# An FFN that takes 512 tokens at a time, with two of its weight matrices streamed from DRAM

## The chip, the core and the metric

The kernel runs on one core of a Trainium2 chip. The metric is the device time of one execution in microseconds (us), lower is better. The engines are TensorE (PE, with its weight loads shown apart as PEld), VectorE (DVE), ScalarE (ACT), GpSimd (POOL) and SyncE (SP), which issues the DMAs here. All inputs are float32.

## What is computed

Two blocks with adaLN modulation follow each other on `x` of shape [4, 2048, 256]. The first is a gated delta-rule memory with 4 heads of 64, which runs over chunks of 64 tokens with a state `S` per head. The second is an FFN with a SwiGLU layer and two GELU layers of width 1024. Its weights are ternary (-1, 0, 1) with a scale per output.

```python
h = _layernorm(x) * (1 + ca) + sa
x = x + ga * memory(h)          # below, per chunk
h = _layernorm(x) * (1 + cb) + sb
x = x + gb * ffn(h)

def step(S, inp):               # one chunk of the memory
    A_i, v_i, wk_i, rkg_i, wkg_i, intra_i = inp
    v_new = A_i @ v_i - (A_i @ wk_i) @ S
    o_i = rkg_i @ S + intra_i @ v_new
    S = gamma_C * S + wkg_i @ v_new

def ffn(x):
    h = silu(lin(x, w1_w, w1_s)) * lin(x, w2_w, w2_s)     # 256 -> 1024
    h = gelu(lin(h, h1_w, h1_s))                          # 1024 -> 1024
    h = gelu(lin(h, h2_w, h2_s))                          # 1024 -> 1024
    return lin(h, w3_w, w3_s)                             # 1024 -> 256
```

`A_i` is the inverse of a unit triangular 64 x 64 matrix of the chunk's keys.

## The kernel before

A step is one chunk of 64 tokens of all four batch elements, so 256 tokens; there are 32 steps. The FFN of step `s` runs beside the recurrence of chunk `s + 1` and the chunk-local matrices of chunk `s + 2`.

All FFN weights lie on the chip in float32r (`fw1`, `fw2`, `fh1`, `fh2`, `fw3`, lines 103 to 107). An activation is kept as two float32r parts whose sum is exactly the activation (`split`, line 366), so every product takes two passes. `Ffn` (line 395) emits a layer in chunks of 128 outputs. `product` (line 425) emits the matmuls of such a chunk: the weights are the stationary operand (128 x 128), the activations stream past with 256 columns. `gated` has 4 + 4 matmuls and puts both products into one PSUM bank; ACT takes Silu of the first (line 441), DVE multiplies (442), and the split is a cast on ACT (367) and a subtraction on POOL (368). `hidden` has 16 matmuls, Gelu on ACT (450), a cast on ACT and a subtraction on DVE. `last` (453) has the activations as the stationary operand and `fw3` streaming with 256 columns. The pool `pf` (line 84) has three PSUM banks for all of these.

The rest of a step is called from the loop over `s` (line 658) at fixed places. `local_keys` makes the keys of chunk `s + 2` and their transposes, `local_grams` the 64 x 64 products; their masked result goes to DRAM and comes back as `U` (lines 248 to 250). `local_inverse` inverts the diagonal blocks of 32 on DVE, 31 times two instructions (258 and 260); `local_blocks` stores the result and loads it as `E` (266, 270). `local_merge1` and `local_merge2` complete the inverse on TensorE. `rec_state`, `rec_values`, `rec_update` and `rec_out` are the recurrence. `ffn_norm` and `ffn_turn` make the input `hs` of the next FFN step, `local_norms` the input of the memory.

Each engine works through its own queue. A planner lays out the queues when the program is built, by its own estimate of when each instruction's operands are ready (line 738). `tc.issue_after(f.end)` keeps what stands under it behind the FFN's last matmul so far on TensorE, and only there. All DMAs are issued by SyncE (`move`, line 144) and so stand in one queue. PSUM has `ps2` with two buffers of two banks, `ps1` with one of two banks, and `pf`.

In the set-up (from line 471) each FFN weight is fetched in pieces of 512 KB (`fetch`, 22 of them, eight buffers), cast to float32r on ACT (line 595), and compared with the original on DVE (`compare`, 526), with a count on TensorE. The flag that comes out picks one of two versions of all steps (line 710): float32r if no weight changed, else float32. Nothing inside this branch can be placed ahead of it. Ahead of it stand the matrices and the recurrence of chunk 0 and the first FFN norm.

Of the kernel before, what the change touches and what calls it, by code (L numbers as in the profile page):

```python
"""Two blocks with adaLN modulation on one core: a gated delta-rule memory over chunks of 64 tokens, and an FFN
(SwiGLU and two GELU layers).

A step is one chunk of 64 tokens of all four batch elements 2*n + b. With tokens on partitions, b has partitions
64b..64b+63 and n lies along the free axis. With features on partitions, head 2*p + h has partitions 64h..64h+63 and
(p, n, b) lie along the free axis. The [64, 64] matrices between the tokens of a chunk lie by [tokens of b, (h, p, n)].

The FFN of a step runs beside the recurrence of the next one and the chunk-local matrices of the one after that.

An FFN weight that float32r holds exactly needs one pass for each of the two float32r parts of an activation, whose  # L10
sum is exactly the activation. Whether all of them are such is found out on the chip; if not, the FFN runs in float32.
"""
# [23 lines left out]
# Columns of the constants: what stays, then what only the set-up needs.  # L36
# [6 lines left out]
def constants():  # L43
    """By the shapes alone: indices and masks over the positions of a tile."""
    i = np.arange(P)
    t = (i % C)[:, None]
    col = np.arange(C)[None, :]
    out = np.zeros((P, NCONST), np.float32)
    out[:, IDENT:IDENT + P] = np.eye(P)
    # Row 4 * n + (partition // 32) of the identity.  # L50
    unit = np.zeros((P, 8, K), np.float32)
    for n in range(8):
        unit[i, n, 4 * n + i // K] = 1.0
    out[:, UNIT:UNIT + 8 * K] = unit.reshape(P, -1)
    out[:, DIFF:DIFF + C] = np.maximum(col - t, 0)
    out[:, STRICT:STRICT + C] = col > t
    out[:, PROW:PROW + C] = np.arange(C)
    out[:, TAIL] = C - 1 - i % C
    return out


def over(ap, dim, n):
    """`ap` with a dimension of n that repeats it."""
# [6 lines left out]
def adaln_block_kernel(ctx: ExitStack, tc: tile.TileContext, x_in, ww, wr, decay, log_alpha, w1, w2, h1, h2, w3, scol,  # L70
# [7 lines left out]
    N = B * C  # L78
# [26 lines left out]
    fh1 = cp.tile([P, NH, HID], FR, name="fh1")  # L105
    fh2 = cp.tile([P, NH, HID], FR, name="fh2")
# [4 lines left out]
    ys = [cp.tile([P, 2, D], F32, name=f"y{n}") for n in range(4)]  # L111
# [16 lines left out]

    nc.vector.memset(half, -0.5)
# [10 lines left out]
    def after(name):  # L140
        """What follows is issued behind what was marked last, on its engine."""
        return tc.issue_after(mark[name])
# [10 lines left out]
    def load(s):  # L153
        for b in range(2):
            move(out=ys[s % 4][C * b:C * b + C],
                              in_=x_in[b::2, s * C:(s + 1) * C, :].rearrange("q t d -> t q d"))

    def moments(x):
        """The mean of each token, and one over its deviation."""
# [11 lines left out]
    def local_norms(s):  # L171
        x, rk = ys[s % 4], rks[s % 2]
# [14 lines left out]
    def local_residual(s, h=None):  # L187
        x, h = ys[s % 4], hid if h is None else h
        # x becomes x + ga * h.
# [4 lines left out]
    def local_keys(s, first=False):  # L194
# [14 lines left out]
        # The write keys, a token behind, with tokens on partitions.  # L209
# [20 lines left out]
    def local_grams(s):  # L230
        IT, NMT = ITs[s % 2], NMTs[s % 2]
        # The heads h are row tiles, each with a bank of its own.
# [20 lines left out]
    def local_inverse(s, j0, j1):  # L253
        """Rows of the inverse of the diagonal blocks of 32: partition (g, block, unit), row 4 * c + g at c."""
# [18 lines left out]
    # E = [[EA, EA NMT EB], [0, EB]], of the blocks of 32.  # L273
# [79 lines left out]
    def rec_out(s, oT):  # L353
        y = ys[s % 4]
# [10 lines left out]
    def split(to, a, eng=None):  # L365
        """`a` is exactly the sum of the two parts of `to`."""
# [3 lines left out]
    def ffn_norm(s, xn=None):  # L370
        y = ys[s % 4]
# [6 lines left out]
    def ffn_turn(s, xn, fp, exact):  # L378
# [4 lines left out]
        hm = ap.tile([P, NK, B, C], F32, tag="hm", name="hm")  # L383
        for k in range(NK):
            for b in range(B):
                nc.scalar.activation(hm[:, k, b, :], tp[:, k, b // 2, C * (b % 2):C * (b % 2) + C], AF.Identity,  # L386
                                     bias=modT[:, k, b:b + 1], scale=modT[:, 2 + k, b:b + 1])
        hm = hm.rearrange("q k b t -> q k (b t)")
        if not exact:
            return hm.unsqueeze(1)  # L390
        hs = fp.tile([P, 2, NK, N], FR, tag="hs", name="hs", bufs=1)
        split([hs[:, 0], hs[:, 1]], hm)
        return hs

    class Ffn:
        """The FFN of step s: `part` emits a chunk of 128 outputs of a layer."""

        def __init__(self, s, hs, fp, exact):
            self.s, self.a, self.fp, self.exact = s, hs, fp, exact
# [3 lines left out]
        def weights(self, w, src, o, n):  # L403
            """The columns of a layer's weights that give outputs o .. o + n."""
            if self.exact:
                return w[:, :, o:o + n]
# [4 lines left out]
        def acts(self, o):  # L411
            if o == 0:
                self.next = self.fp.tile([P, self.parts, NH, N], FR if self.exact else F32, tag="act", name="act")
            to = self.next[:, 0, o, :]
# [4 lines left out]
        def done(self, o, to, eng=None):  # L419
            if self.exact:  # L420
                split([self.next[:, 0, o, :], self.next[:, 1, o, :]], to, eng)
# [3 lines left out]
        def product(self, ps, w, lhs_is_w=True, at=None):  # L425
            k_n = w.shape[1]
            for k in range(k_n):
                for i in range(self.parts):
                    a = self.a[:, i, k, :] if at is None else self.a[:, i, k, at]
                    wk = w[:, k, :]  # L430
                    self.end = nc.tensor.matmul(  # L431
                        ps, lhsT=wk if lhs_is_w else a, rhs=a if lhs_is_w else wk,
                        start=k == 0 and i == 0, stop=k == k_n - 1 and i == self.parts - 1).ins

        def gated(self, o):
            ps = pf.tile([P, 2, N], F32, tag="f", name="ps1")
            for n, (w, src) in enumerate(((fw1, w1), (fw2, w2))):
                self.product(ps[:, n, :], self.weights(w, src, o * P, P))
            to = self.acts(o)
            sg = self.fp.tile([P, N], F32, tag="sg", name="sg", bufs=2)  # L440
            nc.scalar.activation(sg, ps[:, 0, :], AF.Silu, scale=sc[:, 0, o:o + 1])  # L441
            nc.vector.scalar_tensor_tensor(to, ps[:, 1, :], sc[:, 1, o:o + 1], sg, ALU.mult, ALU.mult)  # L442
            self.done(o, to, nc.gpsimd)

        def hidden(self, layer, o):
            w, src = ((fh1, h1), (fh2, h2))[layer]
            ps = pf.tile([P, 2, N], F32, tag="f", name="ps2")
            self.product(ps[:, 0, :], self.weights(w, src, o * P, P))
            to = self.acts(o)
            nc.scalar.activation(to, ps[:, 0, :], AF.Gelu, scale=sc[:, 2 + layer, o:o + 1])  # L450
            self.done(o, to)

        def last(self, n):
            if n == 0:
                self.ps = pf.tile([P, 2, D], F32, tag="f", name="ps3")
            for d in (0,) if self.exact else range(0, D, P):
                w = self.weights(fw3, w3, d, D if self.exact else P)
# [284 lines left out]
```

## Time and profile before

| | |
|---|---|
| median of 3 runs | 1783.98 us (1782.61 to 1785.11) |
| the profiled execution, span | 1783.4 us |
| mean granted TensorE clock | 0.983 |
| FFN matmuls of 256 columns | 11264 (8192 + 2048 + 1024) |
| L450 Gelu, 128x256, on ACT | 512, mean 479 ns |
| L368 subtraction, 128x256, on DVE and on POOL | 512 and 256, mean 471 and 738 ns |
| DMA | 71.93 MB, mean 40 GB/s |
| fetches of h1 and h2 in the set-up, 512 KB each | 16, median 5.6 us to landing |

The profile is of one execution and its times are counted from its first instruction. A line such as L431 is a line of the kernel before. A group gives the busy time of all its instructions, the mean duration of one, and the idle time of the engine just ahead of them with what ended it. Matmuls overlap, so the distance between their starts is less than their duration. In the row of slices, each digit is a share in tenths of one of 40 equal parts of the span. "SPq" is SyncE's queue.

### The profile page before, as it was taken

The page shows a single profiled execution, that of the slowest core. Times are in us where ns is not written, and L with a number is a line of the kernel's source. Part 1 is how long each engine was busy: PE and PEld are TensorE (multiplying, and loading weights), DVE is VectorE, ACT ScalarE, POOL GpSimd, SP SyncE. Part 2 cuts the span into 40 slices and gives each one's busy share as a digit, 9 for nine tenths or more (in the row PEclk, how much of TensorE's full clock was granted, in tenths as well). Part 3 has the DMA queues.
Part 4 walks back from the last instruction along what each step waited for, and adds up shares of the span by engine and source line. Part 5 has one row for each costly group of instructions (what it writes and reads, how often), then busy time and mean ns, then how long its engine had stood idle before and what let it go on. Part 6 is the DMA issues. An engine that isn't in the chain of part 4 may idle for free.

```text
span 1783.4 us, 49902 instructions
## 1 busy us (share of the span) xinstructions
PE 1724.5 (97%) x20372; PEld 1653.5 (93%) x20372; DVE 1162.4 (65%) x3705; ACT 984.0 (55%) x2254; POOL 615.2 (34%) x615
## 2 busy tenths in 40 slices
PE   6489999999999999999999999999999999999998
PEld 3279999999999999999999999999999999999998
DVE  6876767666767666677766667766667776566532
ACT  6245555565555556555656655555655565565554
POOL 3234323334433334442323443333343232344111
PEclk8689999999999999999999999999999999999999
DMA  8311111111111111111111111111111111111100
GB/s 278 98 40 38 27 29 30 39 40 40 28 30 32 31 40 41 40 25 28 31 38 40 40 29 31 34 28 40 40 40 25 28 32 37 41 40 23 24 2 15
DMA packets 142319, 71.93 MB, mean 40 GB/s; under 512 B 112320, under 2 KB 130624, under 8 KB 142080
## 3 DMA queue, kind: packets, MB, share of 16 engines
q1 hardware_dynamic: 142080, 68.65, 15.9%
q8 instruction: 161, 2.64, 0.6%
q14 instruction: 78, 0.64, 0.1%
HBM read 43.44 MB, written 16.78 MB: 34 GB/s over the span
## 4 chain that ended last, share of the span: by engine, by line
PE 88%; DVE 6%; DMA 3%; SPq 1%; issue 1%; POOL 1%; ACT 0%; POOLq 0%; DVEq 0%; ACTq 0%
PE ps L431 70%; PE vp L224 3%; PE V L325 2%; DVE zt L258 2%; DVE Z L260 2%; PE O L314 2%; PE tp L200 1%; SPq L145 1%; PE G L239 1%; PE yp L280 1%; PE O L337 1%; PE R L310 1%; PE ep L293 1%; PE SS L342 1%; PE tpf L382 1%
## 5 line engine op out<-in xcount | busy, mean ns | idle before, releaser
L431 PE MATMUL ps<-act,fh 128*128 128x256 f32 x8192 | 1024.8, 282 | 2.5 <-DVE raw L442 2.2
L431 PEld LDWEIGHTS ps<-act,fh 128*128 128x128 f32 x8192 | 980.1, 188 | 13.6 <-DVE raw L442 2.6
L450 ACT ACTIVATE raw<-ps,sc 128x256 f32<-128x256 f32 x512 | 244.4, 479 | 369.4 <-PE ps L431 322.8
L368 DVE TENSOR_TENSOR act<-raw,act 128x256 fp32r<-128x256 f32 x512 | 234.2, 471 | 170.3 <-ACT act L367 170.2
L367 ACT CAST act<-raw 128x256 fp32r<-128x256 f32 x768 | 311.1, 406 | 34.2 <-DVE raw L442 21.4
L258 DVE TENSOR_TENSOR zt<-Z,U 128x60 f32<-128x60 f32 (+24 forms) x992 | 244.3, 246 | 92.6 <-DMA U<-d 65.8
L431 PE MATMUL ps<-hs,fw 128*128 128x256 f32 x2048 | 256.2, 282 | 5.6 <-DVE raw L442 4.2
L362 POOL TENSOR_TENSOR y<-y,ga 128x512 f32<-128x512 f32 x32 | 41.1, 1284 | 614.9 <-DVE ga L361 614.9
L431 PEld LDWEIGHTS ps<-hs,fw 128*128 128x128 f32 x2048 | 246.3, 189 | 6.8 <-DVE raw L442 4.8
L260 DVE TENSOR_TENSOR Z<-Z,zt 128x60 f32<-128x60 f32 (+24 forms) x992 | 211.5, 213 | 24.2 <-DVE zt L258 0.6
L442 DVE SCALAR_TENSOR_TENSOR raw<-ps,sc,sg 128x256 f32<-128x256 f32 x256 | 123.7, 483 | 153.5 <-ACT sg L441 149.5
L441 ACT ACTIVATE sg<-ps,sc 128x256 f32<-128x256 f32 x256 | 121.9, 476 | 165.8 <-PE ps L431 164.4
L368 POOL TENSOR_TENSOR act<-raw,act 128x256 fp32r<-128x256 f32 x256 | 187.1, 738 | 58.8 <-ACT act L367 42.6
L431 PE MATMUL ps<-fw,act 128*128 128x256 f32 x1024 | 126.8, 281 | 1.2 <-DVE act L368 0.6
L431 PEld LDWEIGHTS ps<-fw,act 128*128 128x128 f32 x1024 | 120.0, 188 | 3.6 <-DVE act L368 0.8
L167 POOL TENSOR_TENSOR rs<-rs,half 128x2 f32<-128x2 f32 x64 | 54.3, 849 | 114.5 <-DVE rs L166 114.5
L386 ACT ACTIVATE hm<-tpf,modT 128x64 f32<-128x64 f32 x256 | 82.4, 417 | 9.7 <-PE tpf L382 9.7
L214 POOL TENSOR_TENSOR wkg<-wkg,gtail 128x512 f32<-128x512 f32 x32 | 33.5, 1047 | 149.5 <-DMA wkg<-rk 105.8
L224 PE MATMUL vp<-wwT,hT 128*128 128x256 f32 x256 | 63.0, 391 | 15.9 <-DVE modT L626 15.4
L191 POOL TENSOR_TENSOR gh<-hid,mod 128x512 f32<-128x512 f32 x32 | 47.4, 1482 | 77.1 <-DVE rn L182 77.0
L464 DVE TENSOR_TENSOR gb<-ps,mod 128x512 f32<-128x512 f32 (+1 forms) x33 | 22.3, 675 | 77.3 <-PE ps L431 77.3
L224 PEld LDWEIGHTS vp<-wwT,hT 128*128 128x128 f32 x256 | 47.8, 196 | 22.0 <-issue 15.5
(208 smaller groups left out, 1640.2 us busy)
## 6 DMA issues: line engine op xcount, KB each, us to landing
U<-d SPq DMA_DIRECT2D x128, 128.0 KB, 2.5
y<-in_x_dram SPq DMA_DIRECT2D x64, 128.0 KB, 9.3
st<-in_h_dram SPq DMA_DIRECT2D x16, 512.0 KB, 5.6
wkg<-rk SPq DMA_DIRECT2D x64, 126.0 KB
out_dram<-y SPq DMA_DIRECT2D x62, 128.0 KB, 2.5
d<-NMT SPq DMA_DIRECT2D x128, 32.0 KB, 4.2
d<-Z SPq DMA_DIRECT2D x128, 32.0 KB, 1.7
E<-d SPq DMA_DIRECT2D x128, 32.0 KB, 2.0
```

Source lines behind the costliest of these rows:

```text
L167: nc.gpsimd.tensor_tensor(rs, rs, half[:, 0:2], ALU.pow)
L191: nc.gpsimd.tensor_tensor(t, h, mod[:, GA], ALU.mult)
L224: nc.tensor.matmul(vp[:, n, :], lhsT=hT[:, k, n, :], rhs=wwT[:, k, :], start=k == 0, stop=k == NK - 1)
L258: nc.vector.tensor_tensor(t[:, 0:n, 0:w], Z[:, 0:n, j:j + 1].to_broadcast([P, n, w]), over(U[:, j, j + 1:K], 1, n), ALU.mult)
L260: mark["inverse"] = nc.vector.tensor_tensor(Z[:, 0:n, j + 1:K], Z[:, 0:n, j + 1:K], t[:, 0:n, 0:w], ALU.add).ins
L367: nc.scalar.copy(to[0], a)
L368: (eng or nc.vector).tensor_tensor(to[1], a, to[0].bitcast(F32), ALU.subtract)
L386: nc.scalar.activation(hm[:, k, b, :], tp[:, k, b // 2, C * (b % 2):C * (b % 2) + C], AF.Identity, bias=modT[:, k, b:b + 1], scale=modT[:, ...
L431: self.end = nc.tensor.matmul(ps, lhsT=wk if lhs_is_w else a, rhs=a if lhs_is_w else wk, start=k == 0 and i == 0, stop=k == k_n - 1 and i ...
L441: nc.scalar.activation(sg, ps[:, 0, :], AF.Silu, scale=sc[:, 0, o:o + 1])
L442: nc.vector.scalar_tensor_tensor(to, ps[:, 1, :], sc[:, 1, o:o + 1], sg, ALU.mult, ALU.mult)
L450: nc.scalar.activation(to, ps[:, 0, :], AF.Gelu, scale=sc[:, 2 + layer, o:o + 1])
```

## The change

The FFN takes the tokens of two steps at a time: `N` becomes 512, and there are 16 pairs instead of 32 steps. The activations then need twice the room, and `fh1` and `fh2` give up theirs. In the set-up their rounded pieces are written to DRAM (`fhs`), laid out so that one chunk of 128 outputs is 4 KB in a row for each partition. `hidden` fetches its chunk of weights into a ring of four tiles of 512 KB.

`gated` puts its two products into a PSUM tile each, with Silu between them. The FFN becomes a generator that yields after every unit of about four matmuls: 16 units of gated, 64 of hidden and 8 of last, so 44 for each half of a pair. `attention(s)` gives, for each half, a list of what runs beside it with the unit from which it may be issued; the recurrence is now that of chunk `s + 2`, the keys and matrices those of chunk `s + 3`, the norms those of chunk `s + 4`. `begin` (blocks and state) stands at the end of a half, behind the last layer at the end of a pair. The whole recurrence of chunk 1, with its inverse, moves ahead of the branch, as do two loads of `x`. `ys` has six buffers.

```diff
-    N = B * C
+    N = 2 * B * C
+    YS = 6
...
-    fh1 = cp.tile([P, NH, HID], FR, name="fh1")
-    fh2 = cp.tile([P, NH, HID], FR, name="fh2")
...
-    ys = [cp.tile([P, 2, D], F32, name=f"y{n}") for n in range(4)]
+    ys = [cp.tile([P, 2, D], F32, name=f"y{n}") for n in range(YS)]
...
+    fhs = [dp.tile([NH, P, NH, P], F32, name=f"fh{n}") for n in range(2)]
...
+        def product(self, ps, w, units):
+            count = w.shape[1] * self.parts
+            for m in range(count):
+                k, i = divmod(m, self.parts)
+                self.matmul(ps, w[:, k, :], self.a[:, k, i, :], m, count)
+                if (m + 1) * units % count == 0 and m < count - 1:
+                    yield
         def gated(self, o):
-            ps = pf.tile([P, 2, N], F32, tag="f", name="ps1")
-            for n, (w, src) in enumerate(((fw1, w1), (fw2, w2))):
-                self.product(ps[:, n, :], self.weights(w, src, o * P, P))
+            pair = []
+            for w, src in ((fw1, w1), (fw2, w2)):
+                ps = pf.tile([P, N], F32, tag="f", name="ps1")
+                w = w[:, :, o * P:o * P + P] if self.exact else self.fetch(src, o * P, P)
+                yield from self.product(ps, w, 1)
+                pair.append(ps)
+                if len(pair) == 1:
+                    sg = self.fp.tile([P, N], F32, tag="sg", name="sg", bufs=2)
+                    nc.scalar.activation(sg, ps, AF.Silu, scale=sc[:, 0, o:o + 1])
+                    yield
             to = self.acts(o)
+            nc.vector.scalar_tensor_tensor(to, pair[1], sc[:, 1, o:o + 1], sg, ALU.mult, ALU.mult)
             self.done(o, to, nc.gpsimd)
+            yield
         def hidden(self, layer, o):
+            ps = pf.tile([P, N], F32, tag="f", name="ps2")
+            if self.exact:
+                w = self.fp.tile([P, NH, P], FR, tag="w", name="w", bufs=4)
+                move(out=w.bitcast(F32), in_=fhs[layer][o])
...
+            yield from self.product(ps, w, 4)
             to = self.acts(o)
+            nc.scalar.activation(to, ps, AF.Gelu, scale=sc[:, 2 + layer, o:o + 1])
             self.done(o, to)
+            yield
...
         for n in range(len(parts)):
-            rounded.append(nc.scalar.copy(parts[n][0].rearrange("q k o -> q (k o)"), staged[n]))
+            to, _, far = parts[n]
+            got = su.tile([P, 1024], FR, tag="got", name="got", bufs=8) if far else to.rearrange("q k o -> q (k o)")
+            nc.scalar.copy(got, staged[n])
+            rounded.append(got)
+            if far:
+                move(out=to.rearrange("o p c -> p o c"), in_=got.bitcast(F32).rearrange("q (o c) -> q o c", c=P))
...
         local_values(1, local_keys(1))
+        load(2)
+        load(3)
...
         rec_out(0, rec_update(0, vn, None))
+        r, O = rec_state(1)
+        local_inverse(1, 0, K - 1)
+        local_blocks(1)
         ffn_norm(0, rks[0])
+        Y = local_merge1(1)
+        local_merge2(1, Y)
+        vn = rec_values(1, r)
+        rec_out(1, rec_update(1, vn, O))
+        ffn_norm(1, v)
     val = nc.values_load(flag, min_val=0, max_val=1)
...
+    HALF = Ffn.UNITS // 2
+    USUAL = dict(load=0, keys=2, grams=9, merge1=9, merge2=13, values=15, update=19, out=24, proj=26, norm=28, turn=32,
+                 norms=35, inverse=(13, 44))
+    FIRST_ = dict(load=0, keys=18, grams=21, merge1=23, merge2=25, values=26, update=29, out=33, proj=34, norm=35,
+                  turn=38, norms=40, inverse=(24, 44))
     def steps(exact):
...
+            hs = new_hs()
+            ffn_turn(0, rks[0], hs, exact)
+            ffn_turn(1, v, hs, exact)
             local_norms(2)
+            local_values(2, local_keys(2))
+            local_grams(2)
+            local_norms(3)
...
+            def begin(l):
+                local_blocks(l)
+                had["r"], had["O"] = rec_state(l)
+            for g in range(NS // 2):
+                f = Ffn(g, hs, fp, exact)
+                units = f.run()
+                next(units)
+                for h in range(2):
+                    s = 2 * g + h
+                    plan = attention(s)
+                    for u in range(HALF):
+                        while plan and plan[0][0] <= u:
+                            with tc.issue_after(f.end):
+                                plan.pop(0)[2]()
+                        next(units, None)
+                    if s + 3 < NS:
+                        with tc.issue_after(f.end):
+                            begin(s + 3)
+                hs = had.get("hs")
```

In the first half of the first pair `attention` also holds the inverse of chunk 2 (from unit 1) and its blocks and state (unit 17). The set-up, the other calls and `last` keep their instructions; `last` is called for both steps of a pair.

## The prediction

> **What bounds the kernel now.** I read the page first (engine shares, slices, chain of waits, costliest groups), then the order of time on TensorE for one steady step, the busy time by stretch, SyncE's own waits, and VectorE in the set-up.
>
> ```profile
> span 1783.4 us, 49902 instructions
> PE 1724.5 (97%) x20372; PEld 1653.5 (93%) x20372; DVE 1162.4 (65%) x3705; ACT 984.0 (55%) x2254; POOL 615.2 (34%) x615
> ...
> PEclk8689999999999999999999999999999999999999
> ...
> PE 88%; DVE 6%; DMA 3%; SPq 1%; issue 1%; POOL 1%; ACT 0%; POOLq 0%; DVEq 0%; ACTq 0%
> ...
> L431 PE MATMUL ps<-act,fh 128*128 128x256 f32 x8192 | 1024.8, 282 | 2.5 <-DVE raw L442 2.2
> ```
>
> TensorE is busy nearly always, carries 88% of the chain, and its largest group waited 2.5 us in all. The 12% that others carry lie in the set-up. A matmul's 282 ns is latency; matmuls overlap, so their price is the distance between starts. The chain in order of time gives it:
>
> ```profile
> 305.37 9.42 PE ps L431 x80
> 316.38 5.67 PE ps L431 x48
> ...
> 357.89 9.42 PE ps L431 x80
> ```
>
> 5.67/48 = 0.118 us for an FFN matmul of 256 columns, and a step of 357.89 - 305.37 = 52.52 us. A step has 352 FFN matmuls (64 gated, 256 hidden, 32 last): 41.5 us. The other 11.0 us are the recurrence, the chunk matrices and the changes between kinds of matmul.
>
> ```profile
> 351.20 1.89 PE L224 MATMUL vp<-wwT,hT 128*128 128x256 f32 x8
> ...
> 305.37:357.89 52.52, 52.52 (x638) 51.09 (x638) 35.01 (x116) 29.69 (x69) 19.11 (x19) 1.00 0.15 34
> ```
>
> The second line is a steady step: busy PE, PEld, DVE, ACT, POOL, then clock 1.00, DMA share 0.15, 34 GB/s. The others have room. The first line prices 512 columns. These 8 are four float32 products, each in two instructions; (1.89 - 0.38, the median duration of one) / 7 = 0.216 us between starts. The transposes (128 columns, also float32; 4 in 0.60) stand (0.60 - 0.28)/3 = 0.107 apart, so such an instruction streams its columns twice, and 512 columns at clock 1.00 cost 0.216.
>
> **What the Trainium skill says.** "TensorE: Matmul & The Clock Gate", section "Back-to-back issue gap", gives N/2.4 + 2.5 ns: 109 for 256 columns, 216 for 512. The trace has 0.216 for 512 streamed columns, but 0.118 for the FFN's 256: there 9 ns more belong to something else, most likely the weight load of each matmul. (The same section's sustained 131 ns for N = 512 lies below the columns' own time, and nothing here supports it.) "SBUF — State Buffer", section "SBUF: two separate sides", says that VectorE and GpSimd lock each other out of a shared port for a whole instruction, VectorE when both its inputs lie in SBUF. The trace agrees: L368's subtraction of 512 elements takes 0.69 alone and 1.78 at 362.82, beside a 1.29 GpSimd addition that began at 362.75. "DMA: Bandwidth & Descriptors", section "Anatomy of one DMA — SWDGE (gpsimd) path", notes that waits on semaphores are held by the issuing sequencer; SyncE's queue shows it:
>
> ```profile
> SPq L145 <- DVE Z L260: 532.2, 31, 23.3
> ...
> SPq L145 <- DMA d<-NMT: 42.1, 63, 3.6
> ```
>
> It sits 17.2 us a step (532.2/31) in front of the stores of the inverse, with whatever is queued behind.
>
> **The change, part by part.**
>
> Wider matmuls. Per pair of steps 640 gated and hidden matmuls of 256 columns become 320 of 512; the 64 last ones stay. If the 9 ns are the weight load, which a 512-column stream covers, the price is 0.216; if they are fixed, 2 x 106.7 (256/2.4, an estimate by that page) + 11.3 = 0.225. I take 0.216. A pair goes from 105.04 to 320 x 0.216 + 64 x 0.118 + 22.0 = 98.7: 6.4 saved, 102 over 16 pairs (56 at 0.225). All of it lies on the path.
>
> Recurrence. One more of it runs before the FFN starts and one less beside it: 11.0 off the loop. TensorE's sum in the loop: before, 32 x 41.5 + 30.5 x 11.0 = 1664 (keys of 30 steps, recurrences of 31); after, 16 x 76.7 + 29.5 x 11.0 = 1551. Check on before: first FFN matmul at 95.2, 1664, and 6.2 from the last matmul (1777.2) to the end give 1765; the missing 18 are losses, 11.5 of them in step 0 (95.2 to 159.2, 64.0 long).
>
> Set-up. Here the change pays.
>
> ```profile
> 73.35 2.53 SPq L145 DMA_DIRECT2D U<-d  x4
> ...
> 91.54 0.19 DVE L258 TENSOR_TENSOR zt<-Z,U 128x31 f32<-128x31 f32 x1 [0.17 <-issue]
> ...
> 95.23 1.01 PE L431 MATMUL ps<-hs,fw 128*128 128x256 f32 x3 [0.70 <-ACT hs L367]
> ```
>
> Before, the inverse of chunk 1 starts at 91.54 and runs beside the first FFN step. After, it, its blocks, the whole recurrence and the norm of chunk 1 stand ahead of the branch, and nothing of the FFN can pass that. U is there by 78.4 (73.35 + 2.53 + 2.5 landing). From then VectorE has five comparisons (6.0), S, ga, flag and norm (4.4) and the inverse (16.5, as the one from 40.4 to 56.9): 105.3. Blocks: 7.05 (stores at 121.08, transpose at 128.13): 112.4. Transpose to xn, link by link from the rows: 13.4, plus 3.6 for hand-overs and the half clock (0.51 from 92 to 102; the same page's first part says that an idle array falls to half): 129.4. Step 0 took 24.5 there (66.88 to 91.38) with comparisons in between, the upper end. One FFN turn is left, 5.8 (91.20 to 97.0): 135.
>
> Rounded weights to DRAM. 16 stores of 512 KB in rows of 512 bytes; each waits on SyncE for its cast, with fetches and small chunk transfers behind it. From 40 to 60 and 80 to 100 the engines are mostly free, and the set-up reached 413 GB/s in one slice: 8.4 MB are 20 us that mostly fit. Some small stores will wait for one: 3, bounds 0 and 10. The loads of chunks 2 and 3 (four issues, 2.9 at 89.08) move ahead of the branch too, where SyncE idles. First FFN matmul: 138 (128 to 152), 43 later.
>
> The ring. 256 loads of 512 KB in rows of 4 KB, 134 MB in some 1640 us: 82 GB/s on top of 34. Issue costs 0.45 each (the fetches of the set-up), 3.6 a half. Four tiles lead by three chunks: 3 x 16 x 0.216 = 10.4 plus inserted work; the set-up's fetches landed in 5.6 under heavier traffic. Cost nil while SyncE's order lets them through; without that, rival C.
>
> ACT, VectorE and GpSimd. A gated chunk lasts 8 x 0.216 = 1.73 instead of 0.94. GpSimd's subtraction grows from 0.74 to 1.29 (a 512-element row, L465), ACT's Silu and cast from 0.88 to about 1.40 (0.26 more each; a 512 cast is 0.66), VectorE's product from 0.48 to 0.69. All shares fall. But one bank now holds one product, so three banks are one and a half chunks: a result must be read within 1.7. The copies of keys (1.2 on ACT) and the masks (1.4 on VectorE) come there; each pushes against about 1 us of slack and stands beside 0.8 to 1.3 of inserted TensorE work.
>
> Ends of layers. The next layer needs chunk 7 after 14 matmuls: 3.0 in a hidden layer, 1.65 in the last, where they stay narrow. The last hidden chunk needs Gelu 0.74, cast 0.66, subtraction 0.69 and hand-overs, 2.4: TensorE waits 0.8 a pair. Before, the state's matmuls (1.6) stood there; now they come after the last layer. With crowding at the banks and E (the second merge and the values are two units, 1.7, apart) I take 2.25 a pair (0.8 to 5): 36. The first half has two inverses and GpSimd's locks, as step 0 had: 10.
>
> Table loads of ACT halve (64 to 32), off the path. The inverse (24.4 from 390.65 to its stores, starting 9 after its matrices) still fits a half of 49.
>
> Sum: 138 + 1551 + 46 + 6 = 1741, against a span of 1783.4. The median of the runs is 1784.0, 0.6 above, so the same number serves.
>
> **Rivals.** B: time goes by the column, 2 x 0.118 = 0.236; the loop gives back 102: 1843. For it: 0.118 is above 0.109. Against: 512 columns at 0.216 in the same trace. C, slower: SyncE's queue. A load of weights ordered behind the stores of an inverse waits with them, 17.2 where SyncE arrives as early as now, while the ring covers about 12: 5 plus landing in a half. For it: those 532 us, and one queue for all transfers. Against: the planner that orders the queues places instructions by its own estimate of when they are ready, so loads should stand ahead. It decides from (1783 - 1741)/30 = 1.4 per half; at half the full price, 2.7, the time is 1822. D: crowding is 4 a pair and the FFN starts at 150: 1741 + 28 + 12 = 1781 in full; by half, 1762.
>
> **How the numbers follow.** A (1741) 0.57, D (1762) 0.18, C 0.17, B 0.08. What a measurement of this kernel can tell is about 0.2%, 3.6 us. Faster holds A and most of D: 0.72; same 0.03; slower C, B and the end of D: 0.25. Best case: start at 128 and losses of 23: 1708. The range goes a little below it and far enough up to leave out the worse half of C and all of B: 1702 to 1805. The forecast's own range is 1708 to 1770.
>
> **What would show it.** Starts of wide matmuls 0.216 apart (0.225: fixed part; 0.236: B). Pairs of 98.7 plus losses, 99.5 to 102. First FFN matmul near 138. TensorE's waits: for act at the last layer about 0.8, for w none; waits for a load of weights in the hidden layers, with SyncE waiting for Z just before, show C. A first FFN matmul past 152, or pairs over 103, prove me wrong.

## The result and the profile after

The changed kernel takes 1861.97 us (median of 4 runs, 1861.2 to 1863.96), the kernel before in the same series 1784.55: ratio 1.0436, 95% interval 1.0422 to 1.0451. It is slower, where 1741 was forecast with a range up to 1805. The page of the changed kernel has these lines in answer to those shown of the kernel before:

```profile
span 1862.2 us, 38430 instructions
...
PE 1736.8 (93%) x15252; PEld 1404.8 (75%) x15252; DVE 1094.9 (59%) x3321; ACT 808.2 (43%) x1454; POOL 585.0 (31%) x487
...
PEclk8669989999999999999999999999999999999999
...
PE 44%; DVE 31%; DMA 12%; SPq 6%; issue 3%; POOL 2%; ACT 1%; DVEq 0%; POOLq 0%; ACTq 0%
...
L436 PE MATMUL ps<-act,w 128*128 128x512 f32 x4096 | 1005.6, 398 | 4.5 <-POOL act L371 4.3
```

With 5120 fewer matmuls TensorE is busy 12 us longer than before (1736.8 against 1724.5). The chain that ended last lies only 44% on TensorE (88% before); VectorE, the DMAs and SyncE's queue carry 49%. Yet the wide matmuls of the hidden layers waited just 4.5 us in all, and those of the gated layer 13.2. So the matmuls themselves must be looked at first. The last pair has no recurrence beside it; TensorE's instructions there, in order of time (start, length, instruction):

```profile
1769.83 14.83 PE L436 MATMUL ps<-hs,fw 128*128 128x512 f32 x64
1784.50 58.21 PE L436 MATMUL ps<-act,w 128*128 128x512 f32 x256
1842.55 5.82 PE L436 MATMUL ps<-fw,act 128*128 128x256 f32 x48
```

From 1784.50 to 1842.55 TensorE has 256 wide matmuls and nothing else: 58.05/256 = 0.227 us each, at a granted clock of 1.00. The median distance of all wide matmuls of the kernel is 0.227 too. The forecast had 0.216.

A steady pair, by the view of busy time in a stretch (length, then PE, PEld, DVE, ACT, POOL busy, clock, DMA share, GB/s):

```profile
813.50:920.70 107.20, 105.52 (x956) 86.24 (x953) 66.31 (x205) 48.38 (x88) 36.20 (x30) 1.00 0.38 112
```

The profiled executions differ by 78.8 us. Where they lie is found by the starts of pairs, that is each pair's first gated matmul, against the starts of every second step before:

| | before | after | difference |
|---|---|---|---|
| first FFN matmul | 95.2 | 141.5 | +46.3 |
| first two pairs (four steps) | 224.8 | 245.4 | +20.6 |
| next 13 pairs (26 steps) | 1367.6 | 1382.9 | +15.3 |
| from there to the last matmul | 89.2 | 84.3 | -4.9 |
| to the end of the span | 6.5 | 8.0 | +1.5 |

From the first FFN matmul to the last, the forecast had 1597 (1551 and 46 of losses) where the kernel before has 1682: 85 were to be given back. The changed kernel takes 1713, 31 more than before.

### The profile page after: what moved, and what is told of

It reads as the page before. It is cut to its first block, busy times and chain, and to the rows that moved or that the text cites. A ratio compares the mean times of both kernels' runs of the same rounds, so it can differ in the third digit from the quotient of the medians.

```text
span 1862.2 us, 38430 instructions
## 1 busy us (share of the span) xinstructions
PE 1736.8 (93%) x15252; PEld 1404.8 (75%) x15252; DVE 1094.9 (59%) x3321; ACT 808.2 (43%) x1454; POOL 585.0 (31%) x487
## 4 chain that ended last, share of the span: by engine, by line
PE 44%; DVE 31%; DMA 12%; SPq 6%; issue 3%; POOL 2%; ACT 1%; DVEq 0%; POOLq 0%; ACTq 0%
PE ps L436 34%; DVE zt L261 9%; DVE Z L263 8%; SPq L148 6%; DMA U<-d 5%; DVE act L371 3%; DMA d<-NMT 2%; DMA E<-d 2%; DMA d<-Z 2%; DVE bs L166 1%; PE tp L203 1%; PE vp L227 1%; DVE gb L493 1%; PE G L242 1%; POOL y L494 1%
## 5 line engine op out<-in xcount | busy, mean ns | idle before, releaser
L436 PE MATMUL ps<-act,w 128*128 128x512 f32 x4096 | 1005.6, 398 | 4.5 <-POOL act L371 4.3
L436 PEld LDWEIGHTS ps<-act,w 128*128 128x128 f32 x4096 | 758.0, 188 | 171.2 <-POOL act L371 9.0
L472 ACT ACTIVATE raw<-ps,sc 128x512 f32<-128x512 f32 x256 | 176.6, 691 | 438.0 <-PE ps L436 421.4
L261 DVE TENSOR_TENSOR zt<-Z,U 128x60 f32<-128x60 f32 (+24 forms) x992 | 244.0, 246 | 157.6 <-DMA U<-d 129.6
L370 ACT CAST act<-raw 128x512 fp32r<-128x512 f32 x384 | 238.9, 623 | 132.2 <-DVE raw L459 123.9
L371 DVE TENSOR_TENSOR act<-raw,act 128x512 fp32r<-128x512 f32 x256 | 184.9, 727 | 170.3 <-ACT act L370 170.3
L436 PE MATMUL ps<-hs,fw 128*128 128x512 f32 x1024 | 263.7, 408 | 13.2 <-ACT hs L370 7.1
L436 PEld LDWEIGHTS ps<-hs,fw 128*128 128x128 f32 x1024 | 189.9, 192 | 63.3 <-DVE gb L493 10.9
L371 POOL TENSOR_TENSOR act<-raw,act 128x512 fp32r<-128x512 f32 x128 | 164.3, 1291 | 108.1 <-ACT act L370 107.9
L459 DVE SCALAR_TENSOR_TENSOR raw<-ps,sc,sg 128x512 f32<-128x512 f32 x128 | 95.8, 749 | 113.5 <-ACT sg L456 64.8
L436 PE MATMUL ps<-fw,act 128*128 128x256 f32 x1024 | 132.0, 284 | 14.0 <-DVE act L371 10.0
L436 PEld LDWEIGHTS ps<-fw,act 128*128 128x128 f32 x1024 | 124.6, 190 | 19.7 <-DVE act L371 12.6
L456 ACT ACTIVATE sg<-ps,sc 128x512 f32<-128x512 f32 x128 | 88.2, 689 | 73.3 <-PE ps L436 72.6
L187 POOL TENSOR_TENSOR rn<-rn,half 128x8 f32<-128x8 f32 x32 | 66.0, 2063 | 13.3 <-DVE rn L186 13.0
```

The lines of the kernel that those rows point to most:

```text
L187: nc.gpsimd.tensor_tensor(rn, rn, half, ALU.pow)
L261: nc.vector.tensor_tensor(t[:, 0:n, 0:w], Z[:, 0:n, j:j + 1].to_broadcast([P, n, w]), over(U[:, j, j + 1:K], 1, n), ALU.mult)
L370: nc.scalar.copy(to[0], a)
L371: (eng or nc.vector).tensor_tensor(to[1], a, to[0].bitcast(F32), ALU.subtract)
L436: self.end = nc.tensor.matmul(ps, lhsT=lhsT, rhs=rhs, start=m == 0, stop=m == count - 1).ins
L456: nc.scalar.activation(sg, ps, AF.Silu, scale=sc[:, 0, o:o + 1])
```

## The experiments

In the tables below "steady" is the mean of eleven pairs, from the start of the fourth to that of the fifteenth; the changed kernel has 106.73 there, two steps before have 105.2. The pairs of one execution lie some 0.5 around their mean, so differences of 0.4 in it say little. The first four kernels below, up to the one with fewer stores, ran once each, the others four times or more.

### What a matmul costs, by itself

Series of 64 matmuls each were put at the end of the kernel before, on operands that lie ready. The granted clock is 1.00 in all of them.

```diff
+        series("r512", rw, rm(512), 512)
+        series("r384", rw, rm(384), 384)
+        series("r256", rw, rm(256), 256)
+        series("r128", rw, rm(128), 128)
+        series("h512", lambda m: rw(m, 64), rm(512), 512, rows=64)
...
+        series("s512", lambda m: rw(0), rm(512, 0), 512)
...
+        series("b512", lambda m: bw[:, m % 8 * P:m % 8 * P + P], lambda m: bm[:, m % 5 * 64:m % 5 * 64 + 512], 512)
```

> The kernel before with eleven series of 64 matmuls behind its end (so its time is not to be compared). Theory A, the price of float32r goes by the column, 17/16 of the clock's time: 0.227 us between starts at 512 columns, 0.170 at 384, 0.113 (or 0.118) at 256; 0.227 also with weights of 64 columns and with one and the same operand; bfloat16 0.216 at 512. Theory B, a fixed part for the weight load: 0.225 at 512, 0.118 at 256, and 0.216 at 512 with half the weight columns. Theory C (the forecast): 0.216 at 512 whatever the type.

The order of time on TensorE; each row joins the series of one letter (r: 512, 384, 256 and 128 columns; h, s and b: 512 and 256):

```profile
1793.55 40.55 PE L724 MATMUL r<-fw,fw 128*128 128x512 f32 x256
1833.94 22.16 PE L724 MATMUL h<-fw,fw 128*64 128x512 f32 x128
1855.93 22.36 PE L724 MATMUL s<-fw,fw 128*128 128x512 f32 x128
1878.14 20.97 PE L724 MATMUL b<-bm,bw 128*128 128x512 bf16 x128
```

The medians of the distances between starts, in ns, from the same trace:

| columns | 512 | 384 | 256 | 128 |
|---|---|---|---|---|
| r: float32r, weights of 128 columns | 227 | 173 | 120 | 111 |
| h: float32r, weights of 64 columns | 230 | | 113 | |
| s: float32r, always the same operands | 227 | | 120 | |
| b: bf16 | 216 | | 109 | |

The rows add up: 64 x (0.230 + 0.113) = 22.0 of 22.16 for h, 64 x (0.216 + 0.109) = 20.8 of 20.97 for b. A narrower weight lowers the price of 256 columns (0.120 to 0.113) and not that of 512, so at 512 the width of the weights doesn't set the price: a float32r matmul of 512 columns costs 0.227 whatever is loaded, and one in bf16 0.216. The DMA share beside these series is 0.01 or less, so the ring isn't the reason either. The part that a wide matmul can save is what is left above half of 0.227: 5 to 7 ns of 118 to 120 for each half.

### The inverse of chunk 1 left out of the set-up

```diff
-        local_inverse(1, 0, K - 1)
```

> The changed kernel without the 62 VectorE instructions that invert the blocks of chunk 1 ahead of the branch (chunk 1 is computed with the identity). Theory A, the serial work of chunk 1 sets the start: first FFN matmul near 126 instead of 141.5, total near 1847. Theory B, the stores of the weights set it: the start stays within 3 us, total 1860.

1830.07 us; first FFN matmul at 117.9, first two pairs 246.6, steady 105.92. The start is 23.6 earlier and the total 32 less. Theory A had 15.5 for the start: VectorE's 62 instructions are on the path that sets the start, in full, and more goes with them than their own time; what, is not shown. Another 9 lie in the eleven steady pairs (0.8 each); nothing in this one run says why.

### The ring loaded once a layer, and fewer stores

```diff
-                w = self.fp.tile([P, NH, P], FR, tag="w", name="w", bufs=4)
-                move(out=w.bitcast(F32), in_=fhs[layer][o])
+                if o == 0:
+                    self.w = self.fp.tile([P, NH, P], FR, tag="w", name="w", bufs=4)
+                    move(out=self.w.bitcast(F32), in_=fhs[layer][o])
+                w = self.w
```

> The changed kernel with one tile of weights loaded for each GELU layer and used for all eight chunks (14 of 16 loads of a pair left out). Theory A, the ring costs TensorE nothing itself: pairs of 106 to 106.8 instead of 106.8, total 1845 to 1862. Theory B, its loads hold up the chunk transfers in SyncE's queue and so VectorE and TensorE: pairs near 104, total near 1810.

14 of a pair's 16 loads are left out, so most chunks use another chunk's weights. 1837.80; start 141.0, first two pairs 239.8, steady 105.36: 24 less in all, between the two theories. The second run has, on top of this, an eighth of the stores of rounded weights:

```diff
-                move(out=to.rearrange("o p c -> p o c"), in_=got.bitcast(F32).rearrange("q (o c) -> q o c", c=P))
+                move(out=to[0], in_=got.bitcast(F32)[:, 0:P])
```

> As the run with one load for each layer, and the 16 stores of rounded weights in the set-up cut to the one chunk of eight that is read. Theory A (the stores mostly fit beside other work): the first FFN matmul 3 us earlier than there, total 3 less. Theory B (the set-up is bound by its transfers, whose share was 0.9 to 1.07 from 20 to 80): 10 to 15 us earlier.

1838.49. The FFN starts at 137.2, 3.8 earlier, and the first two pairs take 4.3 longer: in this pair of runs the stores cost 4 at the start and nothing in the end.

Is it the queue that the ring costs? SyncE's own waits in the changed kernel:

```profile
SPq L148 <- PE ps L436: 713.0, 195, 18.9
SPq L148 <- DVE Z L263: 148.1, 31, 11.8
```

SyncE stands 713 us in front of loads whose slot TensorE has not freed yet, with the small transfers of U and E queued behind. VectorE's waits for those, in the changed kernel:

```profile
DVE Dm L274 <- DMA E<-d: 144.3, 30, 7.2
DVE zt L261 <- DMA U<-d: 129.6, 31, 7.3
```

and with the ring loaded once:

```profile
DVE Dm L274 <- DMA E<-d: 135.3, 30, 6.4
DVE zt L261 <- DMA U<-d: 109.5, 32, 7.3
```

They fall by 9 and 20 and stay far above the 64.5 and 65.8 of the kernel before. Next, the loads were issued by GpSimd:

```diff
-                move(out=w.bitcast(F32), in_=fhs[layer][o])
+                nc.gpsimd.dma_start(out=w.bitcast(F32), in_=fhs[layer][o])
```

> The loads of the ring are issued by GpSimd instead of SyncE; nothing is left out. Theory A (it is SyncE's one queue, in which 713 us are spent waiting for a ring slot with the transfers of U and E behind, that holds VectorE up): VectorE's waits for U and E fall from 7.2 a chunk toward 3, pairs to about 105.2 as with the ring loaded once, total 1838 to 1848. Theory B (the traffic of the loads itself costs the time, through slower landings of the small transfers): waits stay above 6, total 1858 to 1866. Theory C (GpSimd now waits for ring slots ahead of its subtractions): the hidden layer starts late, pairs over 107, total above 1870.

1854.86 (1850.98 to 1858.76): 7 less; steady 106.52. VectorE's wait for E falls to 97.7, that for U stays at 128.3, and GpSimd now waits 427.5 for ring slots. None of the three theories had this: taking the ring out of SyncE's queue gains little by this route. What GpSimd's own waits take back of it isn't known, so the full cost of the shared queue stays open.

### Two orders

Two small waits of TensorE lay in each pair: at the last layer for VectorE's split, and at the first hidden layer for GpSimd's split of the last gated chunk. In the first run the state of the next chunk is issued in the gap ahead of the last layer:

```diff
+                        if h == 1 and u == 35 and s + 3 < NS:
+                            with tc.issue_after(f.end):
+                                had["r"], had["O"] = rec_state(s + 3)
...
```

> The recurrence's first matmuls (state of chunk s + 3) are issued in the last layer's gap instead of behind it; nothing is left out. Theory A (TensorE stands still for 0.89 us a pair in front of the last layer, and only lack of other matmuls there makes it so): that wait falls to 0.2 or less, a steady pair from 106.4 to about 105.6, the total to 1848 to 1853. Theory B (the wait is a symptom, the last hidden chunk is held by its split and the time reappears elsewhere in the pair): pairs stay at 106.2 to 106.6, the total within 3 of 1862.

In the second the inverse's first instruction, which waits for U, is put behind the last gated product on VectorE:

```diff
-                            with tc.issue_after(f.end):
+                            with tc.issue_after(f.end), tc.issue_after(f.prod if u >= 15 else f.end):
```

(`f.prod` is that product; the inverse's first unit is 15 instead of 13.)

> The first instruction of the inverse is put behind the last gated product on VectorE; nothing is left out. Theory A (the wait at the first hidden layer's last chunk, 0.34 to 0.75 a pair, is VectorE standing in front of that product with an inverse that waits for U): the wait goes, 0.4 to 0.75 a pair, total 1850 to 1857. Theory B (the inverse now ends later, and its blocks come later for the merge, so the wait moves to the gated banks of the next half): total 1860 or more.

The third has both.

> Both edits together; nothing is left out. If the two waits are independent: 1.3 to 1.6 a pair, total 1836 to 1844, a steady pair of 105.0. If both only move the same slack, no better than the better one of them alone, about 1850. In either case above the 1784 of the kernel before, since 227 ns a matmul leaves about 2 a pair to be gained and the later start costs 46.

| | total | range | steady |
|---|---|---|---|
| state early | 1845.95 | 1845.24 to 1846.85 | 105.91 |
| inverse behind the product | 1847.47 | 1846.65 to 1848.37 | 105.83 |
| both | 1840.76 | 1838.12 to 1841.35 | 105.39 |

TensorE's waits for the two splits in the changed kernel:

```profile
PE ps L436 <- DVE act L371: 10.0, 13, 0.9
...
PE ps L436 <- POOL act L371: 4.3, 8, 0.8
```

and with both edits:

```profile
PE ps L436 <- DVE act L371: 3.7, 9, 0.5
PE ps L436 <- POOL act L371: 0.8, 1, 0.8
```

Each theory A had the direction, and each gain was a little larger than forecast; together they give 21 instead of 16 + 14.5, inside the 1836 to 1844 that was set for independent waits, though short of their sum. In the eleven steady pairs all of TensorE's recorded waits fall from 14.3 to 3.4 us, 1.0 of the 1.3 by which such a pair gets shorter. So far the mechanism is shown.

### All of it relieved

Both orders, the ring loaded once, and no inverse of chunk 1.

> The changed kernel with both orders mended (state early, inverse behind the product), the ring loaded once a layer and the inverse of chunk 1 left out; left out of the computation: 14 of 16 loads of weights a pair, so most chunks use the wrong weights, and that inverse. If the three gains stand on separate waits they add up: 1862 - 21 - 24 - 32 = 1785. If the mended order and the ring are one slack seen twice: 1800 to 1808. In neither case clearly below the kernel before: at 0.227 a matmul, even the relieved wide loop only pays for its later start.

1814.84: first FFN matmul at 120.0, first two pairs 244.3, steady 105.28. That is 7 above the rival's 1800 to 1808 and far from 1785. On top of the mended orders the ring's relief and the missing inverse together give nothing in a steady pair (105.39 to 105.28), and what is gained beyond them is the start (142.8 to 120.0). So what "ring once" gained alone in the pairs was most likely the same slack: late transfers that reached TensorE through the two waits that the orders remove.

### The second inverse of the first half

```diff
-                    for j in range(K - 1):
-                        plan.append((1 + j // 2, len(plan), lambda j=j: local_inverse(2, j, j + 1)))
```

> The changed kernel with the inverse of chunk 2, which runs in the first half of the first pair ahead of that of chunk 3, left out (62 VectorE instructions; the rest of the computation stays). Theory A (two inverses in one half on VectorE make the second pair's input late and leave TensorE 9 idle before it): the first two pairs fall from 245 by 15 to 25, total 1838 to 1848. Rival B (the first pairs are long because of half clock and of waits behind the stores of the set-up): under 5.

1835.06; first two pairs 227.1 instead of 245.4, total 27 less (3 beyond theory A's bound), of which 18 lie in those two pairs: theory A. The half clock of rival B may have a share in it: the mean granted clock in the two pairs is 0.95 in the changed kernel and 0.97 here, against 0.98 in the four steps of the kernel before. The two go together, and no run parts them. Busy time by stretch, the end of the first pair in the changed kernel:

```profile
255.00:270.00 15.00, 5.72 (x80) 4.04 (x78) 13.74 (x54) 4.21 (x12) 2.96 (x3) 0.78 0.01 2
```

TensorE (the second number) is busy 5.72 of 15 us while VectorE (the fourth) has 13.74. With two inverses in one half VectorE is late with the recurrence, and the next pair's input with it. TensorE's rows there:

```profile
265.18 1.14 PE L386 MATMUL tpf<-kept,xn 128*128 128x128 f32 x4 [3.82 <-DVE xn L378]
269.92 0.80 PE L436 MATMUL ps<-hs,fw 128*128 128x512 f32 x1 [3.60 <-ACT hs L370]
```

### The price in place: the same kernels in bf16

If the price of the matmul is the term that failed, the changed kernel must get back some 57 us when its matmuls do cost 0.216. The same edit was made in both kernels:

```diff
-FR = mybir.dt.float32r
+FR = mybir.dt.bfloat16
```

(with the reads of such tiles as float32 taken out, and `fhs` in bf16).

> The changed kernel with the FFN's weights and both parts of its activations in bf16 instead of float32r: same instructions, same shapes, the same two passes. Changed in the computation: the two parts hold some 16 bits of an activation instead of all of it. The weights in DRAM and the ring have half the bytes. Theory A (the price of the wide matmul is what failed, and TensorE sets the pair): 5120 matmuls fall from 0.227 to 0.216, 57 us, and the 1024 of the last layer from 0.113 to 0.109, 4; half the ring's traffic gives at most half of the 24 that loading it once gave; total 1788 to 1802, a steady pair near 102.5. Rival B (pairs are set by waits and the recurrence, TensorE has slack that a cheaper matmul only adds to): total above 1840.

1796.05 (1795.35 to 1800.92), 66 less than in float32r, within theory A's bounds; ratio to the kernel before 1.0081 (1.0064 to 1.0097), so still far from 1741. The bare last pair:

```profile
1720.33 55.42 PE L436 MATMUL ps<-act,w 128*128 128x512 bf16 x251
1775.59 5.40 PE L436 MATMUL ps<-fw,act 128*128 128x256 bf16 x48
```

(1775.59 - 1720.33)/256 = 0.216 (five records are missing). A steady pair falls from 106.73 to 103.33, by 3.4, and 320 x 0.011 is 3.5. That the two agree so well is in part luck. In the eleven steady pairs TensorE's recorded waits for others grow from 14.3 to 38.2 us, 2.2 a pair, so the rest of its time fell by some 5.6. The rows that grew most (in the whole kernel; 6.3 and 1.8 us in float32r):

```profile
PE ps L436 <- DVE gb L493: 17.0, 16, 2.5
...
PE tp L203 <- DVE rem L320: 15.1, 12, 2.6
```

Other things came along with the type: narrow matmuls of the last layer at 0.109, wide ones that no longer have distances of 0.229 to 0.240 (38 of 100 in the steady pairs in float32r), half the ring's bytes, shorter splits (L371 on VectorE 698 ns instead of 727). The first two pairs take 11.4 less and the start 3.0. So the run shows what the type is worth; what the price of a wide matmul alone is worth, 56, is the sum with the measured 0.227 and 0.216.

With both orders mended as well:

> The changed kernel in bf16 with the two mended orders (state early, inverse behind the product). Theory A (the losses of order are the same as in float32r, 21 in all): 1775, bounds 1765 to 1785, a pair of 101.2. Rival B (with the cheaper matmul VectorE is late at other places, above all at the gated banks, where its wait was 17.0): 1788 or more.

1801.32 (1794.09 to 1810.27), steady 103.16: no gain, rival B. TensorE's largest waits in the pairs are again the two of the last run, 16.5 us behind the recurrence's L320 and 16.2 for the last layer's bank (L493), both on VectorE, which neither order touches.

The kernel before in bf16:

> The same change of type alone in the kernel before, with its 256 columns and its resident weights; the same 16 bits of an activation. Theory A (the price by type that the series showed, 0.109 against 0.113 to 0.120): 11264 matmuls of 0.118 become 0.109, 101 us less; bounds 45 (if only the undisturbed 0.113 goes) and 120; total 1665 to 1740, likeliest 1685. Rival B (a weight load of 128 columns, 0.111 at the least in the series of 128 columns, holds the distance at 0.113 or above): 1730 to 1784.

1854.57 (1847.64 to 1855.51): its matmuls are 0.109 apart (median), as theory A had it, and it is 71 slower. Neither theory had that. A step takes 55.4 instead of 52.6. TensorE's waits and its order of time in one step:

```profile
PE ps L431 <- DVE act L368: 93.4, 28, 4.4
```

```profile
712.25 4.24 PE L431 MATMUL ps<-fw,act 128*128 128x256 bf16 x19 [3.94 <-DVE act L368]
716.27 2.53 PE L431 MATMUL ps<-hs,fw 128*128 128x256 bf16 x16
```

A second cost stands behind the wait. The 19 matmuls behind it take (716.27 - 712.25)/19 = 0.21 us each, twice 0.109: the granted clock from 712.25 to 716.40 is 0.50. From 320 to 1750 its mean is 0.96, an estimate of up to 57 us (0.04 x 1430) beside the 93.4 us of waits. VectorE at that place:

```profile
704.38 1.08 DVE L368 TENSOR_TENSOR act<-raw,act 128x256 bf16<-128x256 f32 x3
711.44 0.45 DVE L271 STREAM_TRANSPOSE Dm<-E 128x256 f32<-128x256 f32 x1 [5.97 <-DMA E<-d]
711.81 0.72 DVE L368 TENSOR_TENSOR act<-raw,act 128x256 bf16<-128x256 f32 x2
```

The transpose of E waits 5.97 for its load and stands ahead of the last two splits, for which the last layer waits. In the next run the blocks go behind the last split (`f.sub`), nothing else:

```diff
-                    local_blocks(s + 2)
+                    with tc.issue_after(f.sub if exact else f.end):
+                        local_blocks(s + 2)
```

> The kernel before in bf16 as in the run e10, with the blocks of the inverse put behind the last split of the second hidden layer on VectorE, so that its transpose, which waits 4.9 a step for E, no longer stands ahead of two splits that the last layer needs. Theory A (the cheaper matmul is real and only that one wait, 93.4 in all, ate it): the wait goes, a step falls from 55 to 49.5 to 50.5 (352 x 0.109 + 11.0 and small losses), total 1690 to 1730. Rival B (VectorE's chain of inverse, store, load and merge is itself the bound at 54 to 55 a step; the wait moves to the merge or to the recurrence): total above 1780.

1731.89 (1724.65 to 1733.88), ratio 0.9697 (0.9671 to 0.9722): faster than both kernels, just above theory A's 1730. Two steps take 102.0. The row of 93.4 is gone from TensorE's waits; the largest in the steps is now 12.6 us in all, and the mean granted clock from 320 to 1640 is 1.00. Its price is precision: an activation is kept to some 16 bits in its two parts, not whole. The same order in float32r:

> The kernel before, in float32r, with the same one order as in e13 and nothing else. Here TensorE never waited for those splits (no such row among its waits). Theory A (at 0.118 a matmul the splits come in time whatever stands ahead of them): within 4 of the kernel before. Rival B (the order has a cost there too, hidden in the 0.118): 5 to 30 faster.

1782.66, ratio 0.9995 (0.9986 to 1.0004): the order is worth nothing there. So it isn't the order alone and not the price alone; the faster matmul needs it.

## Why the prediction was wrong

**The price of a wide matmul: failed.** The step "I take 0.216" failed. It took the price of float32 products for that of float32r, and with it a formula that agreed with them (the Trainium skill, "TensorE: Matmul & The Clock Gate", section "Back-to-back issue gap"), and put the 9 ns above 0.109 down to the weight load. Measured are 0.227 in float32r, and 0.216 only where the FFN is in bf16. Of the 9 ns, 4 (0.113 against 0.109) come with the type, and 11 at 512 columns; only the rest could be saved by wider tiles. 5120 x 0.011 is 56 us of the 121 by which the forecast missed. The prediction's other branch, 0.225, is close by luck: its fixed part for the weight load isn't what the series show. The trace of before had the answer beside the 0.118 that was read from it:

```profile
320.07 1.98 PE L431 MATMUL ps<-hs,fw 128*128 128x256 f32 x16
...
1737.02 5.61 PE L431 MATMUL ps<-hs,fw 128*128 128x256 f32 x48
1742.46 30.25 PE L431 MATMUL ps<-act,fh 128*128 128x256 f32 x256
```

(1.98 - 0.28)/15 = 0.113: twice that is the 0.227 that was then measured. The two rows of the last step, where nothing of another step runs, show that this isn't a matter of being disturbed: (1742.46 - 1737.02)/48 is 0.113 too, but the 256 behind take 0.1175 on average up to 1772.55, the first 47 of them 0.113 and nearly all others 0.118. What moves a stretch from one distance to the other isn't shown. Rival B ("time goes by the column") was right in kind; its size, 0.236, was twice the more frequent of the two, and it had a chance of 0.08, because the float32 row spoke for 0.216.

**Losses: too small, and of another kind.** The pair's sum with the measured price is 98.7 + 3.5 = 102.2; a steady pair takes 106.7, so it loses 4.5 where 2.25 was taken (bounds 0.8 to 5). The wait ahead of the last layer, forecast at 0.8, was there with 0.9. Not forecast were the inverse that waits for U ahead of the last gated product, and that the waits for U and E double (U 129.6 instead of 65.8). But all of TensorE's recorded waits are 14.3 us in the eleven steady pairs, 1.3 a pair (before: 0.5 us in eleven times two steps), and with both orders mended, at 0.3, a pair still takes 105.4. So most of the 4.5 isn't a recorded wait. From each FFN matmul to the one behind it on TensorE, waits taken off, the sum is 4.9 a pair above 320 x 0.227 + 64 x 0.118, where two steps before are 2.4 above 704 x 0.118. These 2.5 are spacing: part of it are the wide distances of 0.229 to 0.240, part may be waits too short to leave TensorE idle. The forecast took all that stands between the FFN's matmuls as the same before and after. In all, the losses cost 35 us more than forecast, and the bound held.

**The first half: failed in size.** Two inverses in it were named and priced at 10. The first two pairs take 245.4, 32 more than two steady ones; leaving one inverse out took 18 of them away. With the 56 and the 35, these 22 beyond the 10 that were priced and 3 at the start make up nearly all of the 121.

**The set-up: right.** 138 was forecast (43 later), 141.5 came (46 later). The transpose to Dm began at 114.70 against the 112.4 of the working; the stores' 3 turned out 3.8 at the start, and nothing in the end. The inverse's share was larger than its 16.5 of instructions: leaving it out moved the start by 23.6 in the one run.

**The ring: half right.** TensorE never waits for w, as forecast, so rival C in its form (a load of weights that comes late) did not happen; SyncE arrives at its loads early. What the forecast did not see is the other direction: SyncE waits 713 us for ring slots, and the small transfers wait behind. Issuing from GpSimd's queue gave 7, loading once 24, and how much of these is the queue alone stays open.

**The marks that were set.** "A first FFN matmul past 152, or pairs over 103, prove me wrong": the second came true.

Price and losses each would have taken the gain of 42 away. With the price of the forecast (the bf16 run, whose waits are its own) the kernel is at 1796, above 1784; with the forecast's losses the measured price gives 1741 + 56 = 1797. Either would have lain inside the range. And the relieved kernel in float32r still takes 105.3 a pair against 105.2 for two steps, so the wide loop has nothing to pay a later start with. What stays open: how much of the wider spacing comes from the changed plan of units, since no run kept the steps' plan with the wide matmuls, and why a stretch of matmuls keeps one distance or the other. The first two pairs' remaining excess was not tried further.

## What to carry to other kernels

Take the price of a matmul from rows of the same type in the same trace, and from several stretches: here one type had two distances, and the float32 row was right for neither. A wider tile saves only what each instruction adds to its columns: ask for that difference, and not for the number of instructions. When TensorE gets cheaper, look at what VectorE has queued ahead of the next operand, and at the granted clock behind each wait: the gain of 52 us in bf16 first showed as a loss of 71.

## What the runs showed of the hardware

- The distance of float32r matmuls of 512 columns is 0.227 us (0.230 with weights of 64 columns); in bf16 it is 0.216. The Trainium skill, "TensorE: Matmul & The Clock Gate", section "Back-to-back issue gap", gives N/2.4 + 2.5 ns, which fits bf16 (0.216 and 0.109) and not float32r: 0.227 is 17/16 of 512/2.4.
- At 256 columns the weights' width matters in float32r: 0.120 with 128 columns, 0.113 with 64. In the kernel before, with 128, stretches of 0.113 and of 0.118 follow each other. At 128 columns the distance is 0.111, nearly that of 256; the weight load may set it there, which wasn't tried. The weight load's mean duration is 188 ns in float32r (L436, act and w) and 98 in bf16.
- Cheaper matmuls can make a program slower: with one order on VectorE the kernel before in bf16 was 71 us slower, with another 52 us faster, than in float32r. In the slower one the granted clock was 0.50 for some 4 us behind a wait of 3.94 us; in the faster one, without these waits, its mean in the steps was 1.00.
